# Second step of a graph layer's segment sums: one-hot matrix as weights, 512 columns streamed, result transposed later

## The chip, the core and the metric

The kernel runs on one core of a Trainium2 chip. The metric is the device time of one execution in microseconds. Before the change it is 2151.89 us, the median of three runs (2151.42 to 2153.22). Five engines work side by side and meet through semaphores: PE does matrix products, DVE and ACT do elementwise work, POOL issues the gathers, and SP issues the plain DMAs.

## The reference

Two graph convolutions of Chebyshev type stand behind a LayerNorm and are added to the input. N = 6250 nodes, D = 512 features, 100000 edges sorted by their destination; everything is fp32.

```python
def _cheb_norm(src, dst, n):
    deg = segment_sum(ones(E), src, num_segments=n)
    dinv = where(deg > 0, rsqrt(maximum(deg, 1.0)), 0.0)
    return -dinv[src] * dinv[dst]
def _cheb_conv(x, src, dst, norm, W0, W1, b):
    out = x @ W0
    tx1 = segment_sum(x[src] * norm[:, None], dst, num_segments=N)
    return out + tx1 @ W1 + b
h = relu(layernorm(x))
h = layer_norm(cheb_conv(h, ..., W1_0, W1_1, b1), gamma, beta)
h = where(h >= 0, h, 0.01 * h)
return x + cheb_conv(h, ..., W2_0, W2_1, b2)
```

The part that the change touches is `tx1 @ W1`. It needs, for each block of 128 nodes, the sum over incoming edges of gathered rows, times minus `dinv` of the destination, and it needs that sum transposed, because a product on PE takes the transposed left operand as its weights.

## The kernel before

**Tiling.** Nodes are cut into NB = 49 blocks of 128 (the last has 106). Edges are cut into NC = 782 chunks of 128. Twelve chunks make a group, and there are NS = 66 groups in each of two layers. The outer loop runs over layers, the inner one over groups `g`.

**The gathers.** Line 380 issues one indirect DMA for each chunk on POOL: 128 rows of 2 KB go from a table in DRAM into one of R = 57 slots of the tile `places`. `gather_to` runs up to 57 chunks ahead of the group that is worked on, and a gather waits until the group that used its slot last is summed.

**First step of the sums.** `sums(g)` (lines 459 to 481) makes one-hot matrices `sel` on DVE (L472) and multiplies them on PE with the gathered rows (L478). Four products of 32 columns each stand side by side in the array. ACT copies the result from PSUM into `agg[g]` (L481, four buffers).

**Second step.** `place(i, some)` (L483 to L496) puts the partial sums of two or three groups where block `i` needs them. DVE makes the one-hot matrix `there` (L491). For each of KD = 4 slices of 128 features PE then takes a slice of `agg` as weights and streams the 128 columns of `there` (L494). The result comes out transposed, as `aT_ps`, and DVE multiplies it by `to` on its way into SBUF as `aT` (L546). `to` is minus `dinv` as a row, copied to all partitions: it is written to DRAM once as `ndinv_d` (L337 to L340), and a 64 KB DMA for each block reads it back 128 times over (L440).

**The dense part.** `own` (L442) transposes the block's own features on PE (L449) and ACT copies them out as `hT` (L451). `dense(i)` (L550) does the products `hT` by W0 and `aT` by W1 (L456, four matmuls each, accumulated in one PSUM bank), and `finish` does the LayerNorm and the stores of layer 0 or the last addition and the store of layer 1.

**Order.** PE, POOL and SP keep the order in which the code is written; ACT and DVE are ordered by a scheduler. In the loop a block that is due is turned (`turn`: own transposes and second step) before `sums(g)`, and its `dense` comes after `sums(g)`:

```python
while inside[i].stop <= g:
    due.append((i, turn(layer, i)))
    i += 1
sums(g)
for k, (hT, aT) in due:
    dense(layer, k, hT, aT)
```

Three groups of four have a block due. At the end of each layer there is nothing to put between: at g = 64 block 47 goes through `turn` and `dense` at once after `sums(64)`; the own products of block 48 and two of its three groups follow; then come `sums(65)`, the third group, and block 48's products with W1. Layer 1 gathers what layer 0's `finish` has stored, so its first gather waits for the last of these stores.

Of the kernel before, what the change touches and what calls it, by code (L numbers as in the profile page):

```python
# [8 lines left out]
F32 = mybir.dt.float32  # L9
BF = mybir.dt.bfloat16  # L10
I32 = mybir.dt.int32
AF = mybir.ActivationFunctionType
OP = mybir.AluOpType
# [6 lines left out]
P = 128  # L20
# [19 lines left out]
def gnn_kernel(  # L40
# [33 lines left out]
    nc = tc.nc  # L74
    N, D = x.shape
    E = src.shape[0]
    NB = -(-N // P)
# [3 lines left out]
    KD = D // P  # L81
# [5 lines left out]
    rows = [min(P, N - i * P) for i in range(NB)]  # L87
# [3 lines left out]
    dram = ctx.enter_context(tc.tile_pool(name="dram", bufs=1, space=bass.MemoryType.DRAM))  # L91
# [4 lines left out]

    tab = [dram.tile([n, D], F32, name=f"tab{i}") for i, n in enumerate((NB * P, N))]
    h_tab = dram.tile([N, D], F32, name="h_tab")
    ndinv_d = dram.tile([NB * P], F32, name="ndinv_d")

    ident = const.tile([P, P], F32, name="ident")
    iota_r = const.tile([P, P], F32, name="iota_r")
    ones = const.tile([P, P], F32, name="ones")
    eps = const.tile([P, 1], F32, name="eps")
    dinv = const.tile([P, NB], F32, name="dinv")
    ndinv = const.tile([P, NB], F32, name="ndinv")
    sdinv = const.tile([P, NB], F32, name="sdinv")
    ln = const.tile([P, 2, NB], F32, name="ln")
    dlx = const.tile([P, 1 + STEP * NQ * NS + 1], F32, name="dlx")
    first = const.tile([P, NQ * NS + 1], F32, name="first")  # L110
    node_of = const.tile([P, NS], F32, name="node_of")
    minus = const.tile([P, 1], F32, name="minus")
# [8 lines left out]
    sc = const.tile([P, 2, NB], F32, name="sc")  # L121
# [180 lines left out]
    with tc.tile_pool(name="turn", bufs=1) as wp, tc.tile_pool(  # L302
        name="turn_ps", bufs=1, space=bass.MemoryType.PSUM
    ) as wps:
        f = wp.tile([P, NG, P], F32, name="f")
        nc.vector.tensor_scalar_add(f, chunks[1], 1.0)
        dl_ps = wps.tile([P, NG * P], F32, name="dl_ps")
        for g in range(NG):
            nc.tensor.transpose(dl_ps[:, g * P : (g + 1) * P], f[:, g, :], ident)
        nc.scalar.activation(dlx[:, 1 : 1 + NC], dl_ps[:, :NC], AF.Copy)  # L310
        down = wp.tile([P, NG, P - 1], F32, name="down")
        nc.vector.tensor_tensor(down, f[:, :, 1:], f[:, :, : P - 1], op=OP.is_lt)
        nc.vector.tensor_reduce(unsorted, down.rearrange("p g e -> p (g e)"), AX.X, OP.add)


        last = ident[:, P - 1 : P]
        first_ps = wps.tile([P, NQ * NS + 1], F32, name="first_ps")
        nc.tensor.matmul(first_ps, last.to_broadcast([P, P]), dlx[:, 0 : STEP * NQ * NS + 1 : STEP], start=True, stop=True)
        nc.vector.tensor_copy(first, first_ps)
        row_ps = wps.tile([P, 2, NS], F32, name="row_ps")  # L320
        for k in range(2):
            for q in range(NQ):
                at = STEP * (q + k)
                nc.tensor.matmul(row_ps[q * Q : (q + 1) * Q, k, :], last.to_broadcast([P, Q]),
                                 dlx[:, at : at + STEP * NQ * (NS - 1) + 1 : STEP * NQ], start=True, stop=True)
        p_i = ep.tile([P, 1], I32, name="p_i")
        p_j = ep.tile([P, 1], F32, name="p_j")
        held = ep.tile([P, NS], F32, name="held")
        nc.vector.tensor_copy(p_i, p_id)
        nc.vector.tensor_single_scalar(p_i, p_i, Q - 1, op=OP.bitwise_and)  # L330
        nc.vector.tensor_copy(p_j, p_i)
        nc.vector.tensor_scalar(node_of, row_ps[:, 0, :], p_j, 1.0, op0=OP.add, op1=OP.add)
        nc.vector.tensor_tensor(held, row_ps[:, 1, :], node_of, op=OP.is_ge)
        nc.vector.tensor_mul(node_of, node_of, held)
        nc.vector.tensor_scalar_mul(minus, last, -1.0)
        rows_ps = wps.tile([NB, P], F32, name="rows_ps")
        nc.tensor.transpose(rows_ps, ndinv, ident)  # L337
        rows_sb = ep.tile([NB, P], F32, name="rows_sb")
        nc.scalar.activation(rows_sb, rows_ps, AF.Copy)
        nc.sync.dma_start(ndinv_d.rearrange("(b p) -> b p", p=P), rows_sb)  # L340

    edges.close()
    unseen = const.tile([1, 1], I32, name="unseen")
# [8 lines left out]

def usual_path(tc, have):
    nc = tc.nc
    (x, out, tab, h_tab, ndinv_d, sidx, dlx, iota_r, w_sb, W2_1, W2_0, w_late, ident, eps, ones, first, node_of, minus,
     unsorted, ln, dinv, sdinv, bias1, bias2, gam, bet, unseen, N, E, D, NB, NC, NU, NS, KD, rows, places, order,
     groups, xs, sc, pick, src_lo, src_hi, p_id, dup) = (
        have[n] for n in ("x out tab h_tab ndinv_d sidx dlx iota_r w_sb W2_1 W2_0 w_late ident eps ones first node_of "
                          "minus unsorted ln dinv sdinv bias1 bias2 gam bet unseen N E D NB NC NU NS KD rows places "
                          "order groups xs sc pick src_lo src_hi p_id dup").split())  # L360
    AHEAD = 2
    ACT = mybir.EngineType.Activation
    R = len(order)
# [3 lines left out]
    with ExitStack() as es:  # L367
# [1 line left out]
        psum = es.enter_context(tc.tile_pool(name="main_ps", bufs=2, space=bass.MemoryType.PSUM))  # L369
        es.enter_context(tc.manual_schedule(engines={PE, POOL, SP}))  # L370
        is_lo, found, looked, gathered = [], 0, 0, RE
        own_h, own_x, to, agg, placed, started, last_hT = {}, {}, {}, {}, {}, {}, {}

        def zr(t):
            return places[:, order[t % R], :]
# [58 lines left out]
        def load(layer, i):  # L434

            own_h[i] = pool.tile([P, D], F32, name="h", bufs=AHEAD)
            for lo, hi in parts(rows[i]):
                nc.sync.dma_start(own_h[i][lo:hi], (h_tab if layer else x)[i * P + lo : i * P + hi, :])
            to[i] = pool.tile([P, P], F32, name="to", bufs=AHEAD + 1)
            nc.sync.dma_start(to[i], dup(ndinv_d[i * P : (i + 1) * P], P))  # L440

        def own(layer, i):  # L442

            h, r = own_h.pop(i), rows[i]
            if layer == 0:
                nc.scalar.activation(h[:r], h[:r], AF.Relu, bias=ln[:r, 1, i : i + 1], scale=ln[:r, 0, i : i + 1])  # L446
            ps = psum.tile([P, KD, P], F32, name="hT_ps")
            for kc in range(KD):
                nc.tensor.transpose(ps[:, kc, :r], h[:r, kc * P : (kc + 1) * P], ident[:r, :r])  # L449
            hT = pool.tile([P, KD, P], F32, name="hT", bufs=1)  # L450
            nc.scalar.activation(hT[:, :, :r], ps[:, :, :r], AF.Copy)  # L451
            return hT

        def products(u_ps, hT, w, r, start):
            for kc in range(KD):
# [27 lines left out]
        def place(i, some):  # L483

            r = rows[i]
            if i not in placed:
                placed[i] = psum.tile([P, KD, P], F32, name="aT_ps", bufs=1)
            for g in some:
                m = Q * min(NQ, NU - NQ * g)
                there = pool.tile([P, P], F32, name="there", bufs=3)  # L490
                nc.vector.tensor_scalar(there[:m, :r], iota_r[:m, :r], node_of[:m, g : g + 1], -(1.0 + i * P),  # L491
                                        op0=OP.subtract, op1=OP.is_equal)
                for kc in range(KD):
                    nc.tensor.matmul(placed[i][:, kc, :r], agg[g][:m, kc * P : (kc + 1) * P], there[:m, :r],  # L494
                                     start=(g == inside[i][0] and kc == 0),
                                     stop=(g == inside[i][-1] and kc == KD - 1))  # L496

        def finish(layer, i, v):
            r = rows[i]
# [32 lines left out]
        def turn(layer, i):  # L532

            r = rows[i]
            if layer == 1:
                own_x[i] = pool.tile([P, D], F32, name="xt")
                for lo, hi in parts(r):
                    nc.sync.dma_start(own_x[i][lo:hi], x[i * P + lo : i * P + hi, :])
                if i == NB - 1:
                    nc.vector.tensor_add(own_x[i][:r], own_x[i][:r], bias2[:r])  # L540
            if i + AHEAD < NB:
                load(layer, i + AHEAD)
            hT = own(layer, i) if i < NB - 1 else last_hT[layer]
            place(i, [g for g in inside[i] if i < NB - 1 or g == NS - 1])
            aT = pool.tile([P, KD, P], F32, name="aT", bufs=1)
            nc.vector.tensor_tensor(aT[:, :, :r], placed.pop(i)[:, :, :r],  # L546
                                    to.pop(i)[:, None, :r].to_broadcast([P, KD, r]), op=OP.mult)
            return hT, aT

        def dense(layer, i, hT, aT):  # L550

            w0, w1 = (w_late[:, 1], w_late[:, 0]) if layer else (w_sb[1], w_sb[0])
            if i < NB - 1:
                started[i] = psum.tile([P, D], F32, name="u_ps")
                products(started[i], hT, w0, rows[i], True)
            u_ps = started.pop(i)
            products(u_ps, aT, w1, rows[i], False)
            finish(layer, i, u_ps)
# [424 lines left out]
```

## Time and profile before

The profiled execution took 2528.77 us (its span is 2527.0 us), against a median of 2151.89 us without the profiler; the difference has to be kept in mind when durations are read.

| what | value |
|---|---|
| median of three runs | 2151.89 us |
| profiled execution, its span | 2528.77 us, 2527.0 us |
| mean granted PE clock | 0.871 |
| first-step matmuls L478 | 4168 records, 750.8 us busy, mean 660 ns |
| own transposes L449 | 392 records, 63.3 us busy, mean 283 ns |
| copies out of PSUM on ACT, L481 and L451 | mean 596 ns and 592 ns |
| one-hot matrices `there` on DVE, L491 | 260, mean 295 ns |
| DMA of `to`, L440 | 98 of 64.0 KB |

A matmul in fp32 stands in the trace as two records of PE (MATMUL) and two of its weight loads (PEld), so one L494 product is two records. PE's busy time counts each record to a modelled end, and records that follow each other closely overlap: the time that a stream really takes is read from start to start. For POOL's gathers the row shows the issue of the descriptors and not the transfer.

### The profile page before, as it was taken

Reading aid. Unit: us, or ns where it says so; the run is one execution under the profiler, and the core shown is the slowest. Engines: PE = TensorE matmul, PEld = TensorE weight load, DVE = VectorE, ACT = ScalarE, POOL = GpSimd, SP = SyncE. Lnnn points to the kernel's source line nnn. Section 1 sums busy time; section 2 is a strip of 40 time slices with the busy share of each in tenths; the row PEclk is TensorE's granted clock in tenths of the full one; section 3 lists DMA queues with packets and bytes.
Section 4 is the critical chain, followed back from the end, with each engine's and each line's share of the span. In section 5 each row is a group of like instructions: output and inputs, shape, how many; then the busy total and the mean of one; then the engine's idle time right before and its main releaser. Section 6 shows DMA issues by size and latency. Waiting matters only on the chain.

```text
span 2527.0 us, 23538 instructions
## 1 busy us (share of the span) xinstructions
PE 1917.3 (76%) x8843; PEld 872.6 (35%) x8843; DVE 677.3 (27%) x1331; ACT 384.6 (15%) x715; POOL 1506.9 (60%) x1577
## 2 busy tenths in 40 slices
PE   4527778788878888878874488777878877778778
PEld 4414333333323333333330133333333333333334
DVE  7923223232323223223330011111111111111111
ACT  7824111111111111111110000000000000000000
POOL 3175666666665666666407576676666666666640
PEclk9767899989988899999985699898888888889889
DMA  9295677667776667677527676776777777777651
GB/s 338 93 348 160 209 215 226 214 216 225 220 217 208 212 217 227 211 220 224 183 77 212 180 224 207 224 215 212 224 220 223 217 211 217 215 220 224 211 183 48
DMA packets 198921, 527.05 MB, mean 209 GB/s; under 512 B 31840, under 2 KB 45995, under 8 KB 198798
## 3 DMA queue, kind: packets, MB, share of 16 engines
q0 software_dynamic: 125120, 410.09, 53.8%
q1 hardware_dynamic: 73678, 115.36, 13.2%
q8 instruction: 71, 1.16, 0.2%
q14 instruction: 52, 0.43, 0.1%
HBM read 474.06 MB, written 51.27 MB: 208 GB/s over the span
## 4 chain that ended last, share of the span: by engine, by line
PE 59%; issue 14%; another core or an unknown queue 14%; POOL 3%; DVE 2%; DMA 2%; ACT 1%; SPq 0%; POOLq 0%; ACTq 0%; DVEq 0%
PE ps L478 24%; PE u_ps L456 23%; PE aT_ps L494 10%; POOL places L380 3%; PE hT_ps L449 2%; DMA h<-in_x_dram 1%; DMA places<-tab,sidx 1%; ACT agg L481 1%; DVE places L391 0%; PE hT_ps L420 0%; DVE places L392 0%; PE u_ps L420 0%; DVE both L426 0%; ACT hT L451 0%
## 5 line engine op out<-in xcount | busy, mean ns | idle before, releaser
L380 POOL DMA_INDIRECT places<-tab,sidx x1504 | 1437.3, 956 | 834.0 <-issue 384.7
L478 PE MATMUL ps<-places,sel 128*32 128x512 f32 x4168 | 750.8, 660 | 187.6 <-issue 139.6
L494 PE MATMUL aT_ps<-there,agg 128*128 128x128 f32 (+2 forms) x2080 | 340.4, 311 | 245.3 <-issue 187.2
L478 PEld LDWEIGHTS ps<-places,sel 128*32 128x32 f32 x4168 | 164.2, 117 | 689.5 <-issue 621.3
L494 PEld LDWEIGHTS aT_ps<-there,agg 128*128 128x128 f32 (+1 forms) x2080 | 303.9, 222 | 273.9 <-issue 205.4
L472 DVE TENSOR_TENSOR sel<-dlx,node 128x512 f32<-128x512 f32 x132 | 92.0, 697 | 772.7 <-remote 532.4
L481 ACT ACTIVATE agg<-ps 128x512 f32<-128x512 f32 x132 | 78.7, 596 | 1080.2 <-remote 645.9
L456 PE MATMUL u_ps<-w,hT 128*128 128x512 f32 (+1 forms) x392 | 188.4, 615 | 10.4 <-issue 8.9
L456 PE MATMUL u_ps<-w,aT 128*128 128x512 f32 (+1 forms) x392 | 181.2, 595 | 16.8 <-issue 15.3
L456 PE MATMUL u_ps<-places,aT 128*128 128x512 f32 (+1 forms) x392 | 180.7, 598 | 7.3 <-issue 6.1
L456 PE MATMUL u_ps<-places,hT 128*128 128x512 f32 (+1 forms) x392 | 182.0, 605 | 4.3 <-issue 3.4
L491 DVE TENSOR_SCALAR there<-iota_r,node_of 128x128 f32<-128x128 f32 x260 | 75.1, 295 | 288.3 <-remote 149.5
L546 DVE TENSOR_TENSOR aT<-aT_ps,to 128x512 f32<-128x512 f32 (+1 forms) x98 | 67.3, 687 | 198.3 <-PE ps L478 153.6
L451 ACT ACTIVATE hT<-hT_ps 128x512 f32<-128x512 f32 (+1 forms) x98 | 58.0, 592 | 382.4 <-remote 183.7
L456 PEld LDWEIGHTS u_ps<-w,hT 128*128 128x128 f32 (+1 forms) x392 | 71.4, 193 | 128.2 <-issue 127.3
L456 PEld LDWEIGHTS u_ps<-w,aT 128*128 128x128 f32 (+1 forms) x392 | 73.4, 189 | 117.6 <-issue 115.9
L456 PEld LDWEIGHTS u_ps<-places,hT 128*128 128x128 f32 (+1 forms) x392 | 70.2, 189 | 119.4 <-issue 118.4
L456 PEld LDWEIGHTS u_ps<-places,aT 128*128 128x128 f32 (+1 forms) x392 | 74.3, 191 | 105.2 <-issue 104.1
L504 DVE TENSOR_TENSOR u_ps<-u_ps,bias 128x512 f32<-128x512 f32 x48 | 33.5, 699 | 282.5 <-issue 99.2
L380 POOL DMA_INDIRECT places<-in_x_dram,sidx x44 | 44.9, 1021 | 96.8 <-ACT places L394 69.9
L509 DVE TENSOR_TENSOR u_ps<-u_ps,bias 128x512 f32<-128x512 f32 (+1 forms) x49 | 34.3, 699 | 200.6 <-PE u_ps L456 83.9
L446 ACT ACTIVATE h<-h,ln 128x512 f32<-128x512 f32 (+1 forms) x49 | 39.7, 813 | 315.2 <-issue 177.6
(128 smaller groups left out, 944.1 us busy)
## 6 DMA issues: line engine op xcount, KB each, us to landing
places<-tab,sidx POOLq DMA_INDIRECT x1504
h<-in_x_dram SPq DMA_DIRECT2D x48, 256.0 KB
tab<-t SPq DMA_DIRECT2D x48, 256.0 KB
h_tab<-g SPq DMA_DIRECT2D x48, 256.0 KB
h<-h_tab SPq DMA_DIRECT2D x48, 256.0 KB
xt<-in_x_dram SPq DMA_DIRECT2D x48, 256.0 KB
out_dram<-t SPq DMA_DIRECT2D x48, 256.0 KB
places<-in_x_dram SPq DMA_DIRECT2D x4, 1792.0 KB
```

Of the source, the lines that this page charges most:

```text
L380: nc.gpsimd.indirect_dma_start(out=zr(t), out_offset=None, in_=x if layer == 0 and t < RAW else tab[layer], in_offset=bass.IndirectOffsetO ...
L446: nc.scalar.activation(h[:r], h[:r], AF.Relu, bias=ln[:r, 1, i : i + 1], scale=ln[:r, 0, i : i + 1])
L449: nc.tensor.transpose(ps[:, kc, :r], h[:r, kc * P : (kc + 1) * P], ident[:r, :r])
L451: nc.scalar.activation(hT[:, :, :r], ps[:, :, :r], AF.Copy)
L456: nc.tensor.matmul(u_ps[:r], hT[:, kc, :r], w[:, kc, :], start=(start and kc == 0), stop=(not start and kc == KD - 1))
L472: nc.vector.tensor_tensor(sel[:, q : q + same, :w, :], of, node[:, q : q + same, None, :].to_broadcast([P, same, w, Q]), op=OP.is_equal)
L478: nc.tensor.matmul(ps[q * Q : (q + 1) * Q, :], sel[:, q, s, :], zr(chunk[q][s]), start=(s == 0), stop=(s == len(chunk[q]) - 1))
L481: nc.scalar.activation(agg[g][: n * Q], ps[: n * Q], AF.Copy)
L491: nc.vector.tensor_scalar(there[:m, :r], iota_r[:m, :r], node_of[:m, g : g + 1], -(1.0 + i * P), op0=OP.subtract, op1=OP.is_equal)
L494: nc.tensor.matmul(placed[i][:, kc, :r], agg[g][:m, kc * P : (kc + 1) * P], there[:m, :r], start=(g == inside[i][0] and kc == 0), stop=(g ...
L509: nc.vector.tensor_add(v, v, bias1[:r])
L546: nc.vector.tensor_tensor(aT[:, :, :r], placed.pop(i)[:, :, :r], to.pop(i)[:, None, :r].to_broadcast([P, KD, r]), op=OP.mult)
```

## The change

The roles of the operands in the second step are swapped: `there` becomes the weights and the 512 columns of `agg` are streamed. The result is not transposed (nodes on partitions), so minus `dinv` can be a scale for each partition in ACT's copy out of PSUM (`prop`). The copy is transposed on PE in `dense`, that is after `sums(g)`, and DVE copies it out as `aT`. The row form of minus `dinv`, its way through DRAM and the 98 loads fall away.

```diff
-        rows_ps = wps.tile([NB, P], F32, name="rows_ps")
-        nc.tensor.transpose(rows_ps, ndinv, ident)
-        rows_sb = ep.tile([NB, P], F32, name="rows_sb")
-        nc.scalar.activation(rows_sb, rows_ps, AF.Copy)
-        nc.sync.dma_start(ndinv_d.rearrange("(b p) -> b p", p=P), rows_sb)
...
-            to[i] = pool.tile([P, P], F32, name="to", bufs=AHEAD + 1)
-            nc.sync.dma_start(to[i], dup(ndinv_d[i * P : (i + 1) * P], P))
...
-            ps = psum.tile([P, KD, P], F32, name="hT_ps")
+            ps, hT = transposed(h, r, "hT", 2)
+            nc.scalar.activation(hT[:, :, :r], ps[:, :, :r], AF.Copy)
+            return hT
+
+        def transposed(h, r, tag, bufs):
+            ps = psum.tile([P, KD, P], F32, name=f"{tag}_ps", bufs=bufs)
             for kc in range(KD):
                 nc.tensor.transpose(ps[:, kc, :r], h[:r, kc * P : (kc + 1) * P], ident[:r, :r])
-            hT = pool.tile([P, KD, P], F32, name="hT", bufs=1)
-            nc.scalar.activation(hT[:, :, :r], ps[:, :, :r], AF.Copy)
-            return hT
+            return ps, pool.tile([P, KD, P], F32, name=tag, bufs=1)
...
-                placed[i] = psum.tile([P, KD, P], F32, name="aT_ps", bufs=1)
+                placed[i] = psum.tile([P, D], F32, name="at_ps", bufs=1)
...
-                for kc in range(KD):
-                    nc.tensor.matmul(placed[i][:, kc, :r], agg[g][:m, kc * P : (kc + 1) * P], there[:m, :r],
-                                     start=(g == inside[i][0] and kc == 0),
-                                     stop=(g == inside[i][-1] and kc == KD - 1))
+                nc.tensor.matmul(placed[i][:r], there[:m, :r], agg[g][:m], start=(g == inside[i][0]),
+                                 stop=(g == inside[i][-1]))
...
-            aT = pool.tile([P, KD, P], F32, name="aT", bufs=1)
-            nc.vector.tensor_tensor(aT[:, :, :r], placed.pop(i)[:, :, :r],
-                                    to.pop(i)[:, None, :r].to_broadcast([P, KD, r]), op=OP.mult)
-            return hT, aT
-
-        def dense(layer, i, hT, aT):
+            prop = pool.tile([P, D], F32, name="prop")
+            nc.scalar.activation(prop[:r], placed.pop(i)[:r], AF.Copy, scale=ndinv[:r, i : i + 1])
+            return hT, prop
+
+        def dense(layer, i, hT, prop):
 
             w0, w1 = (w_late[:, 1], w_late[:, 0]) if layer else (w_sb[1], w_sb[0])
+            ps, aT = transposed(prop, rows[i], "aT", 1)
+            nc.vector.tensor_copy(aT[:, :, : rows[i]], ps[:, :, : rows[i]])
             if i < NB - 1:
                 started[i] = psum.tile([P, D], F32, name="u_ps")
                 products(started[i], hT, w0, rows[i], True)
```

More of the change, by code (lines that the diff above doesn't have):

```diff
@@ L98, in gnn_kernel @@
     h_tab = dram.tile([N, D], F32, name="h_tab")
-    ndinv_d = dram.tile([NB * P], F32, name="ndinv_d")
     ident = const.tile([P, P], F32, name="ident")
@@ L354, in usual_path @@
     nc = tc.nc
-    (x, out, tab, h_tab, ndinv_d, sidx, dlx, iota_r, w_sb, W2_1, W2_0, w_late, ident, eps, ones, first, node_of, minus,
+    (x, out, tab, h_tab, ndinv, sidx, dlx, iota_r, w_sb, W2_1, W2_0, w_late, ident, eps, ones, first, node_of, minus,
      unsorted, ln, dinv, sdinv, bias1, bias2, gam, bet, unseen, N, E, D, NB, NC, NU, NS, KD, rows, places, order,
-     groups, xs, sc, pick, src_lo, src_hi, p_id, dup) = (
-        have[n] for n in ("x out tab h_tab ndinv_d sidx dlx iota_r w_sb W2_1 W2_0 w_late ident eps ones first node_of "
+     groups, xs, sc, pick, src_lo, src_hi, p_id) = (
+        have[n] for n in ("x out tab h_tab ndinv sidx dlx iota_r w_sb W2_1 W2_0 w_late ident eps ones first node_of "
                           "minus unsorted ln dinv sdinv bias1 bias2 gam bet unseen N E D NB NC NU NS KD rows places "
-                          "order groups xs sc pick src_lo src_hi p_id dup").split())
+                          "order groups xs sc pick src_lo src_hi p_id").split())
     AHEAD = 2
@@ L371, in usual_path @@
         is_lo, found, looked, gathered = [], 0, 0, RE
-        own_h, own_x, to, agg, placed, started, last_hT = {}, {}, {}, {}, {}, {}, {}
+        own_h, own_x, agg, placed, started, last_hT = {}, {}, {}, {}, {}, {}
         def zr(t):
```

## The prediction, made before the result was known

> **What bounds the kernel now.** I read the page's busy times and its costliest groups first, then the timeline of a stretch in which POOL never pauses, then the chain of waits at the end of a layer.
>
> ```profile
> span 2527.0 us, 23538 instructions
> PE 1917.3 (76%) x8843; PEld 872.6 (35%) x8843; DVE 677.3 (27%) x1331; ACT 384.6 (15%) x715; POOL 1506.9 (60%) x1577
> ...
> L380 POOL DMA_INDIRECT places<-tab,sidx x1504 | 1437.3, 956 | 834.0 <-issue 384.7
> L494 PE MATMUL aT_ps<-there,agg 128*128 128x128 f32 (+2 forms) x2080 | 340.4, 311 | 245.3 <-issue 187.2
> L494 PEld LDWEIGHTS aT_ps<-there,agg 128*128 128x128 f32 (+1 forms) x2080 | 303.9, 222 | 273.9 <-issue 205.4
> L546 DVE TENSOR_TENSOR aT<-aT_ps,to 128x512 f32<-128x512 f32 (+1 forms) x98 | 67.3, 687 | 198.3 <-PE ps L478 153.6
> ```
>
> By busy time PE leads, and this misleads twice: the records overlap, and the profiled execution is 375 us longer than the median. The timeline early in layer 1 shows where the extra time sits:
>
> ```profile
> 1393.33 0.95 POOL L380 DMA_INDIRECT places<-tab,sidx  x1 [0.30 <-issue]
> 1393.50 0.37 PE L494 MATMUL aT_ps<-there,agg 128*128 128x128 f32 x1 [2.43 <-issue]
> 1394.20 0.29 PEld L494 LDWEIGHTS aT_ps<-there,agg 128*128 128x128 f32 x1 [1.82 <-issue]
> 1394.59 0.95 POOL L380 DMA_INDIRECT places<-tab,sidx  x1 [0.30 <-issue]
> 1395.61 0.37 PE L494 MATMUL aT_ps<-there,agg 128*128 128x128 f32 x1 [1.74 <-issue]
> 1395.84 0.95 POOL L380 DMA_INDIRECT places<-tab,sidx  x1 [0.30 <-issue]
> ```
>
> Two things are to be seen. POOL issues a gather every 0.95 + 0.30 = 1.25 us and waits for nothing; it holds this pace for 70 gathers on end. PE passes one record in 0.7 to 1.4 us, again with no releaser ("issue"), although these records follow each other at 0.12 us elsewhere. Once the gathers are over (2466 to 2520 us) PE has no such gaps, and the groups that start at 2466.3, 2479.2 and 2489.8 us are some 12 us apart; amid the gathers it is 17.3 us (twelve gathers at the 1.44 us that they take on average there). I take the gaps to be the recording's own: they appear only where gathers crowd the DMA, and the run without a profiler is shorter by about as much as PE is idle in these stretches (900 - 738 from 300 to 1200 us and 900 - 708 from 1400 to 2300 us, together 354 us).
>
> Without the gaps a group costs PE about 11 us: sums 3.6, and for three groups of four own transposes 0.5, second step 2.4, dense 6.9. POOL needs 12 x 1.25 = 15.0 us for its twelve gathers. So POOL's issue is the bound of the unprofiled run, with PE some 4 us per group ahead. The sum: gather 60 starts at 175.0 us; 722 more gathers in layer 0 take 902.5; from the start of the second-last group to the end it is 37.2 us (2489.8 to 2527.0); the same again, with 977.5 us of gathers, for layer 1. 175 + 902.5 + 37.2 + 977.5 + 37.2 = 2129.4, with 1.8 us outside the span 2131 us. The median is 2152; POOL's waits between 189 and 290 us (7.3, 3.5, 10.5, 3.1 and 4.1) would more than fill the difference. In the profiled time, 2528.77 us, the same sum stands with 1.44 us per gather.
>
> The two ends of the layers are PE's, since no gather is left:
>
> ```profile
> 2493.86 2.84 PE L494 MATMUL aT_ps<-there,agg 128*128 128x128 f32 x24
> 2496.54 3.60 PE L456 MATMUL u_ps<-places,hT 128*128 128x512 f32 x8
> 2510.00 1.90 PE L478 MATMUL ps<-places,sel 128*32 128x512 f32 x4
> 2511.94 0.59 ACT L481 ACTIVATE agg<-ps 32x512 f32<-32x512 f32 x1 [7.37 <-PE ps L478]
> 2512.58 1.14 PE L494 MATMUL aT_ps<-there,agg 32*128 32x106 f32 x8 [0.68 <-ACT agg L481]
> 2513.75 0.60 DVE L546 TENSOR_TENSOR aT<-aT_ps,to 128x424 f32<-128x424 f32 x1 [4.71 <-PE aT_ps L494]
> 2514.40 5.38 PE L456 MATMUL u_ps<-places,aT 128*106 128x512 f32 x8 [0.69 <-DVE aT L546]
> ```
>
> Block 47's products follow its second step with no gap, because `hT` is ready; for block 48 each step waits for the one before.
>
> **What the Trainium skill says.** "Perfetto Trace Analysis", section "DMA Instruction — SWDGE (GPSIMD)": the profiled end of such an instruction is the end of descriptor generation, not of the transfer. The trace agrees: 0.95 us each, whatever else runs. The same page, "Identifying the Most-Contended Engine": a matmul's busy share is no measure of how near PE is to its limit. It agrees too: PE is 76% busy over the span, and without gathers beside it a group takes 12 us instead of 17.3. "TensorE: Matmul & The Clock Gate", "Step-by-step: what each phase is for": the next weights load while the running matmul streams, and a stream is paid by its columns. Here a 512-column record takes 0.43 us in a stream (eight from 1717.76 to 1721.19 us), a 128-column one 0.1175 (sixteen from 1721.63 to 1723.51), a transpose 0.11 (four from 1721.19 to 1721.63). "VectorE: DVE Perf Modes", "Mode 2×_2P": PSUM has one read port, so the mode that takes the port DVE shares with GpSimd needs SBUF operands. The new DVE copy reads PSUM and should not slow POOL; the only copy out of PSUM here (128x196, 340 ns) shows no such mode.
>
> **The change part by part.**
>
> *Second step on PE.* There are 260 pairs of group and block. Each was 8 records of 0.1175 = 0.94 us and becomes 2 of 0.43 = 0.86: 21 us less in all. *New transposes:* 98 x 4 x 0.11 = 43 us more. PE's work grows by 22 us in 2150, 0.2 us per group against 4 us of slack: nothing on the path. If that cover were gone it would cost the 22 us.
>
> *New ACT copy `prop`.* 98 x 0.60 us (the rows of L451 and L481). In the loop it runs beside `sums(g)`, 3.6 us, and is needed only after it. ACT is 15% busy: hidden. Behind it on ACT stand the copy of the next `agg` and, in layer 0, `t` and `g`; all of them come later on PE anyway.
>
> *DVE.* The multiply by `to` (0.69 us) goes; a copy of the same size from PSUM comes. No row shows it; below it is bounded by ACT's 0.60, above by the multiply's 0.69. I take 0.65. It runs while PE does the own products (3.43 us), so either end is hidden, except for block 48.
>
> *DMA and SP.* The 98 loads of 64 KB go, 6.4 of 527 MB, and one store with them. They lie beside the gathers. Bounds: 0, as gathers here wait for their issue; or down to 21 us gained, all that lies above POOL's sum. I take 0.
>
> *Start.* One PE transpose and one ACT copy (0.27 us, just before ACT's first table rows at 97.40 us) go: 0 to 0.45 us gained, taken 0.3. From 189 to 290 us POOL waits for PE, ACT and DVE; four blocks then bring 0.44 us of transposes and a later `aT` each. Bounds 0 and 4 us lost, taken 1.
>
> *End of each layer.* Block 47: the second step takes 6 x 0.43 = 2.58 us instead of 2.68 (the chain's value for its 24 records), 0.10 less; then PE waits for the end of the last record (0.16), the hand-overs (0.06) and ACT (0.60), and transposes for 0.44: +1.16 us. Block 48: two pairs, 1.77 to 1.72; the pair of 32 rows, 1.15 us before in 8 records of 106 columns, becomes 2 of 512, between 1.0 and 1.9 by the clock granted, taken 1.3; ACT 0.59 and hand-overs 0.06; transposes and hand-over 0.6, as for its own (2503.41 to 2504.04); the DVE copy replaces the multiply at 0.6. That is +1.35 (1.1 to 2.0). Together 2.5 us, in two layers 5.0 (4.5 to 6.3).
>
> Sum: 5.0 - 0.3 + 1.0 = +5.7 us; 2151.9 + 5.7 = **2157.6 us**, 0.26% slower.
>
> **The rivals.** *A, as summed:* own range 2154 to 2163. About 0.2%, 4.3 us, is what a measurement of this kernel can tell from no change, so A's lower part counts as no change. *B, absorbed:* if the clock is better at the ends, or the dropped loads and the shorter second step give back 3 to 5 us in the head, 2152. For it speaks how small the sum is; against it that the chain shows no idle time at the ends that could take it up. *C, faster:* PE's gaps are partly there without a profiler too. They are paid per record, and PE loses 260 x 12 = 3120 matmul and load-weight records and gains 98 x 8 = 784. Then part of the 21 us above POOL's sum goes: 2152 - 17 = 2135 (2131 to 2147). It cannot be more while 1.25 us per gather stands. Against it: the match of POOL's sum with the median leaves little to gain. *D, slower by more:* PE is the bound after all, and the 22 us come whole beside the ends: 2151.9 + 22 + 5.7 = 2180. It decides as soon as PE's group takes over 15.0 us instead of 11; against it, no stretch without gathers shows this.
>
> **How the numbers follow.** A 0.58, B 0.13, C 0.19, D 0.10. Slower: 0.42 of A and D, 0.52; same: 0.16 of A and B, 0.29; faster: 0.19. The range of 2139 to 2167 takes in A, B and half of C.
>
> **What would show it.** The profile after should have 392 transposes of `prop` near 0.11 us apart in a stream, 520 records of L488 at 0.43, POOL's 1.25 us unchanged, and at 47 and 48 a gap on PE of some 0.8 us before the transposes. With 2336 records fewer on PE, its span should be shorter than 2527 us, even by hundreds, while the median hardly moves. I am wrong if the median falls or rises by over 15 us: then POOL's issue was not the bound.

## The result and the profile after

The changed kernel takes 2157.56 us, the median of seven runs (2154.98 to 2161.54). The kernel before, run beside it, takes 2150.25 us (2148.8 to 2153.22, seven runs too). The ratio is 1.0031 with a 95% interval of 1.0021 to 1.0041: slower by 0.3%, as forecast, and by more than the 0.2% that can be told from no change.

Five lines of the page of the changed kernel answer to those of before (busy us, mean ns of one, then idle time before it and what ended it):

```profile
span 2153.1 us, 20955 instructions
PE 1807.7 (84%) x7674; PEld 679.5 (32%) x7674; DVE 669.9 (31%) x1331; ACT 457.0 (21%) x812; POOL 1513.4 (70%) x1577
...
L374 POOL DMA_INDIRECT places<-tab,sidx x1504 | 1442.0, 959 | 496.6 <-issue 334.2
L473 PE MATMUL ps<-places,sel 128*32 128x512 f32 x4168 | 718.8, 673 | 267.7 <-DMA places<-tab,sidx 253.8
...
L488 PE MATMUL at_ps<-agg,there 128*128 128x512 f32 x520 | 242.3, 598 | 1.4 <-ACT agg L476 1.4
```

Read beside the page of before, this seems to say that the change took 374 us from the profiled span while the median rose. It says nothing of the kind, as run e8 below shows. What holds here is the last number of L473: PE waits 253.8 us for gathered rows, so PE is not the bound. POOL (L374) issues its gathers back to back, 1.25 us from start to start (the median of layer 1).

Where the time went is read at the end of a layer. The chain of waits of the changed kernel in layer 1, from the end of the sums of group 64 (start us, us, what):

```profile
2116.97 0.59 PE hT_ps L446 x4
2117.55 2.59 PE at_ps L488 x6
...
2120.17 0.70 ACT prop L539
...
2120.91 0.65 PE aT_ps L446 x4
2121.57 6.87 PE u_ps L451 x16
...
2137.39 1.12 PE at_ps L488 x2
...
2138.53 0.70 ACT prop L539
...
2139.27 0.60 PE aT_ps L446 x4
...
2139.89 0.61 DVE aT L546
...
2145.79 0.69 DVE t L498
```

The same stretch of the kernel before, from run e8 (a profile of it with the same pace of gathers):

```profile
2117.78 0.59 PE hT_ps L449 x4
2118.36 2.68 PE aT_ps L494 x24
2121.04 6.87 PE u_ps L456 x16
...
2136.91 1.15 PE aT_ps L494 x8
...
2138.08 0.61 DVE aT L546
...
2144.01 0.69 DVE t L505
```

In the old form block 47's products stand directly behind its second step. In the new form ACT's copy (0.70) and the transposes (0.65) stand between them. Block 48 gains the same two steps. From the end of the sums of group 64 to the last DVE instruction before it took 2144.01 - 2117.78 = 26.23 us, and after it takes 2145.79 - 2116.97 = 28.82 us: 2.6 us more. In layer 0 the end of the same sums and DVE's first instruction on block 48's finished products lie 24.7 us apart before (1094.16 to 1118.85) and 27.3 us after (1094.50 to 1121.80): again 2.6. Both ends together cost 5.2 us of the 7.3 between the medians. The interval of the ratio is 4.5 to 8.8 us, so 5.2 alone would fit it; the traces don't say where the other 2.1 us would lie.

### The profile page after: what moved, and what is told of

It reads as the page before. It is cut to its first block, busy times and chain, and to the rows that moved or that the text cites. A ratio compares the mean times of both kernels' runs of the same rounds, so it can differ in the third digit from the quotient of the medians.

```text
span 2153.1 us, 20955 instructions
## 1 busy us (share of the span) xinstructions
PE 1807.7 (84%) x7674; PEld 679.5 (32%) x7674; DVE 669.9 (31%) x1331; ACT 457.0 (21%) x812; POOL 1513.4 (70%) x1577
## 4 chain that ended last, share of the span: by engine, by line
PE 38%; DMA 29%; POOL 16%; issue 12%; DVE 4%; ACT 1%; POOLq 0%; SPq 0%; ACTq 0%; DVEq 0%
DMA places<-tab,sidx 28%; PE u_ps L451 18%; POOL places L374 15%; PE ps L473 12%; PE at_ps L488 4%; PE aT_ps L446 2%; PE hT_ps L446 1%; DVE hi L246 1%; DVE lo L246 1%; PE both_ps L252 1%; DVE places L385 0%; ACT places L425 0%; DMA places<-in_x_dram 0%; DMA places<-in_x_dram,sidx 0%; DVE places L386 0%
## 5 line engine op out<-in xcount | busy, mean ns | idle before, releaser
L374 POOL DMA_INDIRECT places<-tab,sidx x1504 | 1442.0, 959 | 496.6 <-issue 334.2
L473 PE MATMUL ps<-places,sel 128*32 128x512 f32 x4168 | 718.8, 673 | 267.7 <-DMA places<-tab,sidx 253.8
L473 PEld LDWEIGHTS ps<-places,sel 128*32 128x32 f32 x4168 | 142.8, 117 | 819.7 <-DMA places<-tab,sidx 555.2
L488 PE MATMUL at_ps<-agg,there 128*128 128x512 f32 x520 | 242.3, 598 | 1.4 <-ACT agg L476 1.4
L451 PE MATMUL u_ps<-places,aT 128*128 128x512 f32 (+1 forms) x392 | 177.8, 596 | 0.7 <-DVE aT L546 0.7
L451 PE MATMUL u_ps<-places,hT 128*128 128x512 f32 (+1 forms) x392 | 177.5, 596 | 0.7 <-ACT hT L440 0.7
L451 PE MATMUL u_ps<-w,hT 128*128 128x512 f32 (+1 forms) x392 | 177.3, 595 | 0.7 <-ACT hT L440 0.7
L451 PE MATMUL u_ps<-w,aT 128*128 128x512 f32 (+1 forms) x392 | 176.3, 592 | 0.7 <-DVE aT L546 0.7
L488 PEld LDWEIGHTS at_ps<-agg,there 128*128 128x128 f32 x520 | 92.3, 193 | 82.2 <-issue 71.6
L374 POOL DMA_INDIRECT places<-in_x_dram,sidx x44 | 44.1, 1002 | 96.2 <-ACT places L388 66.0
L451 PEld LDWEIGHTS u_ps<-places,aT 128*128 128x128 f32 (+1 forms) x392 | 74.8, 191 | 95.2 <-issue 94.3
L451 PEld LDWEIGHTS u_ps<-w,aT 128*128 128x128 f32 (+1 forms) x392 | 74.3, 190 | 94.3 <-issue 93.4
L486 DVE TENSOR_SCALAR there<-iota_r,node_of 128x128 f32<-128x128 f32 x260 | 82.4, 317 | 62.6 <-PE at_ps L488 62.3
L451 PEld LDWEIGHTS u_ps<-places,hT 128*128 128x128 f32 (+1 forms) x392 | 71.2, 192 | 71.8 <-issue 71.0
L451 PEld LDWEIGHTS u_ps<-w,hT 128*128 128x128 f32 (+1 forms) x392 | 70.9, 191 | 71.8 <-issue 71.0
L539 ACT ACTIVATE prop<-at_ps,ndinv 128x512 f32<-128x512 f32 (+1 forms) x98 | 67.3, 687 | 114.6 <-PE at_ps L488 113.1
```

The costliest lines, as they stand in the source:

```text
L374: nc.gpsimd.indirect_dma_start(out=zr(t), out_offset=None, in_=x if layer == 0 and t < RAW else tab[layer], in_offset=bass.IndirectOffsetO ...
L451: nc.tensor.matmul(u_ps[:r], hT[:, kc, :r], w[:, kc, :], start=(start and kc == 0), stop=(not start and kc == KD - 1))
L473: nc.tensor.matmul(ps[q * Q : (q + 1) * Q, :], sel[:, q, s, :], zr(chunk[q][s]), start=(s == 0), stop=(s == len(chunk[q]) - 1))
L488: nc.tensor.matmul(placed[i][:r], there[:m, :r], agg[g][:m], start=(g == inside[i][0]), stop=(g == inside[i][-1]))
L539: nc.scalar.activation(prop[:r], placed.pop(i)[:r], AF.Copy, scale=ndinv[:r, i : i + 1])
```

## The experiments

The first four ran on one chip, where the kernel before takes 2151.64 us (72 runs).

**e1: is the new copy on DVE to blame?** In the changed kernel it becomes the multiply that DVE did before, by ones.

```diff
-            nc.vector.tensor_copy(aT[:, :, : rows[i]], ps[:, :, : rows[i]])
+            nc.vector.tensor_tensor(aT[:, :, : rows[i]], ps[:, :, : rows[i]],
+                                    ones[:, None, : rows[i]].to_broadcast([P, KD, rows[i]]), op=OP.mult)
```

> The changed kernel, with the DVE copy of aT out of PSUM written as a multiply by a tile of ones (same shape as the multiply by `to` before). Theory 1 (of the 7 us lost, about 5 are the longer chains at the ends of the two layers and the rest is the new copy, beside which POOL's gathers take longer): the time falls by 2 to 4 us against the changed kernel, to about +3 to +5 us over before, ratio about 1.002, and no gather is lengthened beside L546 any more. Rival (all of it is the two ends, as predicted, and the copy costs nothing): the time stays at +5 to +8 us over before, ratio 1.003. Rival 2 (the copy is no cause, and the multiply is slower or keeps DVE longer): the same or slower.

Measured: 2156.77 us, ratio to before 1.0025 (1.0016 to 1.0033). This overlaps the changed kernel's own interval, so no cost of the copy is shown. With 5.1 us over before it lies where the first theory's range ends and the rival's begins: the run does not decide between them.

**e2: are the two ends the whole loss?** Blocks 47 and 48 keep the old second step and the multiply by `to`; the other 47 blocks have the new form.

```diff
-                nc.tensor.matmul(placed[i][:r], there[:m, :r], agg[g][:m], start=(g == inside[i][0]),
-                                 stop=(g == inside[i][-1]))
+                if i < NB - 2:
+                    nc.tensor.matmul(placed[i][:r], there[:m, :r], agg[g][:m], start=(g == inside[i][0]),
+                                     stop=(g == inside[i][-1]))
+                else:
+                    at = placed[i].rearrange("p (k c) -> p k c", k=KD)
+                    for kc in range(KD):
+                        nc.tensor.matmul(at[:, kc, :r], agg[g][:m, kc * P : (kc + 1) * P], there[:m, :r],
...
```

> The changed kernel, with the last two blocks of each layer (47 and 48) in the form of before: weights from `agg`, result transposed at once, multiplied by `to` on DVE. All other blocks keep the new form. Theory 1 (ends 5 us, copy 2 to 4 us): +2 to +4 us over before, ratio 1.001 to 1.002. Rival (all is the ends): back to before within 1 us, ratio 1.000. Rival 2 (the ends cost nothing, the loop is slower): stays at +6 to +8 us, ratio 1.003.

Measured: 2151.73 us, ratio 1.0000 (0.9992 to 1.0009). With the ends undone nothing is left that these runs can tell: the other 94 uses of the new form, 47 blocks in two layers, cost less than 2 us together and bring less than 2 us. (The row form of minus `dinv`, its way through DRAM and 4 of the 98 loads are back with the ends.)

**e3: both edits at once.**

> Both edits at once: the last two blocks in the old form, and the copy of aT in the other blocks written as a multiply by ones. Theory 1 (ends and copy are the whole loss): the time of before within 1 us, perhaps 1 us less, ratio 0.9995 to 1.0005. If something else in the new loop costs time (the 22 us more of PE work, the ACT copy): 2 us or more above before, ratio over 1.001.

Measured: 2151.15 us, ratio 0.9997 (0.9988 to 1.0007), the same as e2. The kind of DVE instruction in the loop makes no difference that these runs can tell.

**e4: what were the dropped loads worth?** The kernel before with one load of `to` in place of 98. Every block is then scaled by block 0's row.

```diff
-            to[i] = pool.tile([P, P], F32, name="to", bufs=AHEAD + 1)
-            nc.sync.dma_start(to[i], dup(ndinv_d[i * P : (i + 1) * P], P))
+            if "all" not in to:
+                to["all"] = pool.tile([P, P], F32, name="to", bufs=1)
+                nc.sync.dma_start(to["all"], dup(ndinv_d[0:P], P))
```

> The kernel before, with the row tile `to` loaded once in each run from block 0 and used for all blocks, instead of 98 loads of 64 KB (the scale of the other blocks is thereby another one). Theory 1 (gathers wait for their issue on POOL, and DMA is not the bound): the time of before within 1.5 us, ratio 0.9993 to 1.0007. Rival (the dropped DMA traffic is worth something and hides a larger loss of the change): 5 to 20 us less than before, ratio 0.990 to 0.998.

Measured: 2152.69 us, ratio 0.9999 (0.9990 to 1.0008). The loads were worth nothing, within the 2 us that these runs can tell.

**e5 to e7** were to test the bound: three times the transposes, fewer gathers, and work moved out of the ends. They ran on another chip, and there the kernel before takes 2533.63 us (27 runs, 2526.53 to 2540.0), without a profiler.

e5, the changed kernel with the transposes of `prop` made three times:

```diff
+            if i < NB - 2:
+                for _ in range(2):
+                    again = psum.tile([P, KD, P], F32, name="aT_ps", bufs=1)
+                    for kc in range(KD):
+                        nc.tensor.transpose(again[:, kc, :], prop[:, kc * P : (kc + 1) * P], ident)
```

> The changed kernel, with the four transposes of `prop` issued three times for every block but the last two of each layer: 94 x 8 x 0.11 = 83 us more of PE work inside the loop. Theory 1 (POOL's issue of the gathers bounds the loop, PE has slack of some 3 us per group): within 2 us of the changed kernel, ratio to before 1.003 to 1.004. Rival (PE bounds the loop): 60 to 83 us slower than the changed kernel, ratio about 1.035.

e6, the changed kernel without 110 of its gathers:

```diff
+                if t >= 120 and t % 12 == 6:
+                    continue
```

> The changed kernel, with one gather of twelve left out from chunk 120 on in both layers (110 of 1564; the products run as before, on the rows that lie in the slot from earlier). Theory 1 (1.26 us of POOL's time for each gather is the bound): 110 x 1.26 = 139 us less than the changed kernel, about 2019 us, ratio to before 0.939, unless PE becomes the bound before that. Rival (PE or latency is the bound): less than 30 us gained, ratio over 0.985.

e7, the kernel before with the own work of blocks 47 and 48 moved to group 63, and two of block 47's groups placed before the sums of group 64:

```diff
+                if g == NS - 3:
+                    ahead(layer, NB - 2)
+                if g == NS - 2:
+                    place(NB - 2, inside[NB - 2][:-1])
                 sums(g)
...
+                if g == NS - 3:
+                    ahead(layer, NB - 1)
```

> The kernel before, with work of the last two blocks moved ahead of the last groups, where PE waits for gathers: block 47's own transposes and products go before the third-last group's sums, block 48's after them, and block 47's first two pairs of the second step before the second-last group's sums (one PSUM bank more for u_ps, one buffer more for hT). Theory 1 (the end of each layer is a chain on PE, and time before it is free): the chain from the end of the second-last group's sums falls from 26 us to about 15, the sums begin up to 2 us later, so 14 to 22 us less than before in two layers, about 2132 us, ratio 0.990 to 0.9935. Rival (the ends are not on the path, or the moved work delays the last sums by as much): within 3 us of before.

Measured, each against before on that chip: e5 2732.63 us, ratio 1.077 (1.0728 to 1.0813). e6 2433.41 us, ratio 0.9593 (0.9564 to 0.9623). e7 2537.5 us, ratio 1.0017 (1.0008 to 1.0025). None met its expectation, and the waits show how this chip differs. Those of PE in e7 (us in total, times, longest; "issue" stands where the trace names nothing that was waited for, no releaser):

```profile
PE aT_ps L494 <- issue: 194.6, 173, 13.7
PE ps L478 <- issue: 137.4, 167, 2.3
```

One of ACT's in e7:

```profile
ACT h L446 <- issue: 184.7, 24, 8.6
```

And one of POOL's in e5:

```profile
POOL places L374 <- PE ps L473: 429.9, 102, 19.1
```

On this chip PE has the gaps without a releaser that the prediction saw in the profile of before, and e7's profiled execution (2537.55 us) takes as long as the median of its runs. POOL waits for PE to free its slots, 429.9 us in e5 and 106.5 us at the same place in e7. But PE is not the only engine that pauses: ACT does, as shown, and DVE has 75.4 and 56.0 us of such waits in e7 before its two additions of the bias. So POOL's pace alone does not set the time here; which engine does was not tested. e6 shows that fewer gathers still help: it takes 100 us less than before. e7 lost 3.9 us. A reason that fits is that PE has little idle time left to fill: it waits 26.7 us for gathers in the whole of e7, against 267.4 us in e8 below. How long the changed kernel itself takes on this chip was not tried: with 2336 records fewer on PE it may be the faster of the two there, and what e5 and e6 cost or gain against it stays open too.

**e8 to e11** repeat the question with controls, with an expectation for either kind of chip. They ran on a chip where before takes 2155.07 us (29 runs).

e8, the kernel before, unchanged:

> The kernel before, unchanged, for its profile on this chip. Theory 1 (PE's gaps belong to the chip or its condition, not to the recording): the profiled span is within 0.3% of this chip's unprofiled median, whichever that is: near 2150 us with few gaps on PE and gathers back to back, or near 2530 us with the gaps. Theory 2 (the prediction's: the recording makes the gaps of this form): the span is some 2530 us while the unprofiled median is near 2150 us.

Its page, and the first of its waits on PE:

```profile
span 2151.1 us, 23538 instructions
...
L380 POOL DMA_INDIRECT places<-tab,sidx x1504 | 1443.6, 960 | 493.8 <-issue 331.5
```

```profile
PE ps L478 <- DMA places<-tab,sidx: 267.4, 182, 13.2
```

Same program, same 23538 instructions, and the profiled span is 2151.1 us instead of 2527.0. PE waits for gathers. Of the gaps without a releaser at L494 and L478, 187.2 and 139.6 us in the profile of before, nothing is left; the only such wait on PE is one of 0.6 us. So the recording alone doesn't make the gaps, and on the chip of e5 to e7 the kernel before takes 2533.63 us with no recording at all. The profile of before and the timed runs beside it came from different conditions. Another chip is the likely one, but no trace tells on which chip that profile was taken. The 374 us between the pages of before and after are a difference between these conditions and no effect of the change. Against this page the changed kernel's span is 2.0 us longer in its first profile and 9.3 us longer in e9's (2160.4 us). Single executions scatter that much (2150.04 to 2160.14 us for before on this chip), so neither measures the change.

e9, the changed kernel, unchanged:

> The changed kernel, unchanged. Where before takes about 2150 us: 2155 to 2158 us, ratio 1.002 to 1.004. Where before takes about 2530 us, theory 1 (there the gaps bind, and they are paid for each record on PE): 2336 records fewer of some 18000 at about 380 us of gaps give 50 us less or more than that, 2430 to 2490 us, ratio 0.96 to 0.985. Rival (there something else binds, such as the gathers' transfer): no change, 2525 to 2540 us.

Measured: 2162.19 us, ratio 1.0027 (1.0020 to 1.0035). The ratio is as expected; the time is above 2158 us, as the kernel before is slower on this chip too.

e10, e5's kernel again:

> The changed kernel with the transposes of prop in blocks 0 to 46 made three times, 1504 more of 0.11 us, 0.88 us per block with one due and 83 us in all. Where before takes about 2150 us: theory (POOL's issue of gathers binds, PE has some 4 us of slack per group): within 4 us of the changed kernel, ratio to before 1.002 to 1.005. Rival D (PE binds): 60 to 83 us more, ratio 1.03 to 1.04. Where before takes about 2530 us: 2733 us again, as on the other chip, 200 to 300 us more than the changed kernel.

Measured: 2156.55 us, ratio 1.0008 (0.9996 to 1.0020). The 83 us of added transposes cost nothing. (They are 752 of 0.11 us; the 1504 in the expectation is a slip.) Its first wait on PE shows where they lie:

```profile
PE ps L473 <- DMA places<-tab,sidx: 181.0, 102, 12.8
```

In e9 this wait is 255.0 us. It shrank by 74 us, most of the 83 added. That PE binds on this chip (rival D) is excluded. The time is 5.6 us under e9's, outside the 4 us expected. The traces hold a possible reason: 36 gathers of e10 take over 1.15 us to issue and 53 of e9, in sum 13.1 and 20.1 us beyond 0.95 us each. What runs beside such gathers is told below; no run tested it.

e11, e6's kernel again:

> The changed kernel without every twelfth gather from chunk 120 on, 110 of 1564 left out (their edges are then summed from the rows that an earlier gather left in the slot, so part of the segment sum is not computed). Where before takes about 2150 us: theory (POOL's issue binds): 110 x 1.25 = 137 us less than the changed kernel, 2015 to 2030 us, ratio 0.938 to 0.944, unless PE takes over on the way. Rival (PE binds): no change, ratio 1.000 to 1.004. Where before takes about 2530 us: 2433 us again, and at most 20 us less than the changed kernel, since there PE binds.

Measured: 2019.41 us, ratio 0.9378 (0.9363 to 0.9394), 142.8 us under e9 where 137 were expected. Each gather left out gives 142.8 / 110 = 1.30 us, about one period of POOL. The gathers' pace binds here. The edit takes away a gather's issue and its transfer together; that the issue sets the pace is read from the traces, where POOL starts a gather every 1.25 us (median) and waits at most 0.3 us for a slot once the first 135 us are over.

**e12: a version that beats both.** If PE waits for gathers up to the last groups, own work of blocks 47 and 48 that stands in the ends can be done in these waits. The kernel before, with that work at groups 58 and 60:

```diff
+                if g == NS - 10:
+                    for k in (NB - 2, NB - 1):
+                        load(layer, k)
+                if g in (NS - 8, NS - 6):
+                    ahead(layer, NB - 2 if g == NS - 8 else NB - 1)
                 sums(g)
...
-                    last_hT[layer] = own(layer, i)
-                    started[i] = psum.tile([P, D], F32, name="u_ps")
-                    products(started[i], last_hT[layer], w_late[:, 1] if layer else w_sb[1], rows[i], True)
```

> The kernel before, with the own transposes and the own products (W0) of block 47 done before the sums of group 58 and those of block 48 before the sums of group 60, in both layers, instead of after the sums of group 64. Theory (the two ends are PE's, and just ahead of them PE waits for gathers, 0.35 + 0.48 + 1.21 + 1.97 + 2.17 + 2.81 = 9.0 us from 2053 to 2091 us): 0.4 + 3.4 us of block 47 and 0.4 + 0.7 + 3.7 us of block 48 leave each end, the first lies in these waits, so 14 to 17 us less where before takes about 2150 us, ratio 0.992 to 0.9935. Rival (the last gathers come later when PE frees the slots later, or the single u_ps bank makes PE wait for DVE): 0 to 6 us less, ratio 0.997 to 1.000. Where before takes about 2530 us PE has no such waits: within 5 us of before, ratio 0.998 to 1.002.

Measured: 2135.69 us against 2149.0 us of before on that chip, ratio 0.9941 (0.9928 to 0.9955). Its chain of waits in the end of layer 1:

```profile
2111.95 2.89 PE aT_ps L501 x24
2114.87 0.70 DVE aT L555
2115.61 3.70 PE u_late L463 x8
2119.31 1.77 PE aT_ps L501 x16
...
2130.83 0.69 DVE t L512
```

From the end of the sums of group 64 to the last DVE instruction it is 2130.83 - 2111.95 = 18.88 us, against 26.23 in e8. Block 47's own work is gone from it, and so is block 48's. In exchange, block 47 now waits for DVE's `aT`, which the own products used to cover. The gain of 13.3 us is a little under the 14 to 17 expected: the estimate counted the work moved and not this wait. In layer 1 the end is 7.35 us shorter; in layer 0 POOL's wait for the last store falls from 35.2 us (e8) to 29.7 us, 5.5 less. The single `u_ps` bank does make PE wait for DVE, as the rival said (20.7 us in 15 waits), and the gain stands all the same.

## Why the prediction was right, and what of it was not

**The ends of the layers: right, and they are the whole effect that these runs can tell.** 5.0 us were forecast, 5.2 are in the chains, and e2 shows that undoing the ends removes the loss to within 2 us. By block: for 47 +1.16 was forecast, and its end moves from 10.13 us (2117.78 to 2127.91) to 11.46 us (2116.97 to 2128.43), +1.33. The terms that were small are ACT's `prop`, 0.70 instead of 0.60, and the transposes with their hand-over, 0.65 instead of 0.44 and a hand-over. On the other side, the 0.16 us put down for the end of the last record don't appear: the copy starts 0.02 us after the 2.59 us of the six records. The price of `prop` could have been read from the profile of before, in another copy of ACT out of PSUM with a scale for each partition; the rows that the prediction took, L451 and L481, have no such scale:

```profile
L522 ACT ACTIVATE t<-u_ps,sdinv 128x512 f32<-128x512 f32 (+1 forms) x49 | 33.6, 687 | 137.7 <-DVE u_ps L519 61.8 <-issue 47.3 <-DVE there L491 20.5
```

For block 48 +1.35 was forecast and it is 2.6 - 1.33 = 1.3; the pair of 32 rows takes 1.12 us, under the 1.3 taken and inside its bounds. The granted clock was 1.00 there. It fell only after that: the eight records of the last products take 5.22 us at a mean clock of 0.70, and 3.68 us at 1.00 earlier in the chain.

**The number: in part luck.** 2157.6 us were forecast and 2157.56 measured. But the sum was 5.7 us on a time before of 2151.9, and measured are 7.3 us (4.5 to 8.8) on 2150.25; the two differences cancel.

**PE's group is hidden behind POOL's issue: right.** The net 22 us of second step and transposes don't show (e2), and even 83 us more don't (e10). This is the step that carries the forecast, and e11 confirms its other half, the gathers' pace. The slack was put too high, though: PE was to be some 4 us per group ahead, and in e8 it is idle for 103.4 of the 750 us from 300 to 1050 us and for 104.2 from 1300 to 2050 us, about 2.1 us for each group of 15.2 us. That is still ten times the 0.2 us per group that the change adds.

**"I take the gaps to be the recording's own": wrong.** This is the step that failed. e8 records the same program without the gaps, and on the chip of e5 to e7 the same program is as slow without a recording. The argument was that the time missing from the median (375 us) is about PE's idle time in the stretches with gathers (354 us). That match is a coincidence: in e8 PE is idle for 207.6 us in stretches with about as many records (6230 against 6451), so the idle time fell by some 147 us and not by 354. The forecast survived because it needed only that the gaps were absent from the timed runs. The test that the prediction named for itself, a span "shorter than 2527 us, even by hundreds", came out as foretold for a reason other than the one given.

**The floor and what lies above it: right in size, wrong in place.** The sum of 2131 us left 21 us, which the prediction put down to POOL's waits between 189 and 290 us. After 131 us the trace of e8 has two waits of POOL over 0.4 us: the one between the layers and one of 0.7 us in layer 1. What is above the floor is the gathers themselves: from gather 58 on, layer 0's 725 follow at 1.266 us on average and layer 1's 782 at 1.264, not at 1.25. That is 725 x 0.016 + 782 x 0.014 = 22.5 us. Most of it (14.7 us) lies in 41 lengthened gathers, as the next paragraph tells.

**The DVE copy should not slow POOL: right as far as the traces go, but gathers are longer beside other work of DVE.** The prediction read 0.95 us for a gather "whatever else runs". In e8 41 of the 1504 gathers take over 1.15 us, and in the changed kernel 50, 14.7 and 17.7 us beyond 0.95 us each. Two instructions of DVE both run during every one of them: `sel`, the one-hot matrices of the first step, and `node`, from which they are made. In the new form the copy mostly lies next to these two:

```profile
202.13 0.69 DVE L467 TENSOR_TENSOR sel<-dlx,node 128x512 f32<-128x512 f32 x1 [3.39 <-PE ps L473]
...
202.37 1.27 POOL L374 DMA_INDIRECT places<-tab,sidx  x1 [0.30 <-issue]
...
202.74 0.68 DVE L546 COPY aT<-aT_ps 128x512 f32<-128x512 f32 x1
...
203.34 0.28 DVE L458 TENSOR_TENSOR node<-first,iota_r 128x128 f32<-128x128 f32 x1
```

So the 108 gathers beside the copy take 1069 ns on average, where the 115 beside the old multiply took 949 ns. But the only four that run beside the copy without `node` or `sel` take 945 ns, and in e1, with a multiply in the copy's place, 44 gathers are lengthened, 28 of them beside it. Four gathers are few, but nothing here points to the copy itself. This agrees with what the prediction took from the Trainium skill ("VectorE: DVE Perf Modes", section "Mode 2×_2P"), and the copy's 0.61 us at block 48, equal to the multiply's, shows no faster mode. e1 and e3 find no difference in time either. That `node` and `sel` lengthen the gathers is read from these traces; no run moved them.

**Loads, start and head.** The loads were put at 0, and e4 says 0 within 2 us. For start and head together 0.7 us was added. e2 has the new form in the head, but the old start, and stands at 1.0000 within 0.0009; neither term is large enough to be told from 0 by these runs.

**Rivals.** D fell (e10). B, absorbed, is excluded by the interval, whose lower end is 1.0021. C needs PE's gaps, and in the traces of the changed kernel, e1 to e4 and e8 to e12 there are hardly any (one of 0.6 us in each). On e5's chip its ground exists, and it was not tried there with the changed kernel alone.

## What to carry to other kernels

Before a profile's durations are used, compare its span with the median of the timed runs; if they differ by 17% as here, find out which of the two conditions the forecast is for, and don't blame the recorder without a second profile. Work added to an engine that waits for another's pace is free up to that wait and costs in full where the other has run out: here, of 98 uses of a longer chain, only the four at the ends of the layers were seen to cost, where no gather is left to wait for. The same view shows where to gain: work in the tail that depends on nothing late belongs in the last waits ahead of it (13.3 us here, against 5 lost by the change).

## What the runs showed of the hardware that was not expected

The same program takes about 2150 us on some chips and 2534 us on another, each within 0.4% of its median there. On the latter PE, ACT and DVE stand still again and again with no releaser while gathers are running: 194.6 us at one line of PE and 184.7 us at one of ACT in e7, and DVE as told above, against 0.6 us on all of PE, 1.3 us on all of ACT and nothing on DVE in e8. In the profile of before, which looks the same, records of PE (weight loads counted) come 0.7 to 1.4 us apart in such stretches. POOL's gathers keep their 1.25 us (median), and after the last of them PE keeps its usual pace. What makes the gaps was not found. A lower granted clock alone does not: its mean is 0.84 to 0.87 in these traces and 0.92 to 0.93 in the others, but from 300 to 1200 us of the profile of before it is 0.92, and the gaps are there. The order of two variants may depend on the chip: what these runs say of the changed kernel holds for the former kind.
